# Normed rows from ScalarE with a scale and a bias per token, block 0's weights from VectorE, later counts, and a sigmoid made from exp

## The chip, the cores and the metric

The kernel runs on one core of a Trainium2 chip. The metric is the device time of one execution in microseconds; a time stands for the median of several runs. A profile is one more execution, recorded by the hardware profiler. Engines are TensorE (PE; PEld is its weight load), VectorE (DVE), ScalarE (ACT), GpSimd (POOL) and SyncE (SP, here a DMA queue).

## The reference

Eight batches of 512 tokens of 256 numbers run through four layers, each added to its input after a layer norm without weights. All is float32.

```
x = x + scan(norm(x))         # xi = silu(x @ Win + b); h = 0.9 h + xi B; y = h C + D xi; y @ Wout + b
x = x + mixture(norm(x))      # router, 16 experts, 4 chosen of each token, and two shared experts
x = x + attention(norm(x))    # 16 heads of 16, causal, scores clipped to +-10, softmax
x = x + mixture(norm(x))

# the router of a mixture:
scores = sigmoid(x @ router_w.T); s = scores + bias
group_score = sum of the 2 best of each group of 4 experts; keep the 2 best groups
topk_idx = the 4 best of s among them; tw = 2.5 * scores[topk_idx] / sum
# an expert: (silu(x @ gate) * (x @ up)) @ down, weighted by tw and summed
```

Tokens of one batch are four tiles of 128 (one token per partition). `norm` is `(x - mean) / sqrt(var + 1e-5)`.

## The kernel before, in words

The program has four stretches in time: the scan stretch (0 to about 373 us), the first mixture's routed experts (to about 770), the attention stretch (to about 1352) and the second mixture's routed experts (to 1752, then the last rows are summed and stored).

A stretch (`stretch`, L1236) goes over the batches. For each batch it issues the layer's main work (`Scan`, L492 on: `pz_s`, the input product L500, sigmoid L509, the products L510 and L513, the recurrence `state_s` L512, `y_s` L516, then `py_s`, the output product L454, which L463 adds to `x`; or `Attention`, from L1013: `pq_a`, `pv_a`, the scores `ps_a` L1096, exp by ScalarE L1107, the clip L1110 and L1118, `po_a` L1131, `pto_a` L1147). Beside the main work of batch b it issues pieces of other batches, each at a share of the main work's columns (`timed`, `spread`): the normed rows and transposes of the next batch's layer input, the routing of batch b-1 (`Route`), the shared experts of batch b-2 (L958 `pg_m`, L972 to L978, L987 `pd_m`), and the scatter of batch b-2's rows into `xg`, ordered by expert. A scheduler then orders each engine's instructions; the order of before and after is fixed when the program is built, and each engine works through its own in order. SyncE's queue carries the loads and stores, GpSimd's queue the indirect scatters.

The names that matter:

- `normed` (L405): statistics per tile (L412, L413 on VectorE), the reciprocal root `rstd` (with `by_vector`, for batches 0 and 1 of the scan layer, for the last batch's routed rows and for the attention inputs that are made beside the first mixture's blocks, by twelve small steps on VectorE, L420 to L428; else an addition on VectorE, L431, and a power on GpSimd, L432), then four rows (L437, VectorE: subtract the mean, times `rstd`). The rows are `xn` (a layer's input) or `sorted_m` (a mixture's rows, which also hold the weights and the destination).
- `turned` (L385): eight transposes by TensorE (L397) into PSUM, `pt_l` or `pt_m`, and two copies to SBUF (L399), `xT_l` or `xT_m`; in the scan layer both copies are ScalarE's.
- the router: `logits` (`pl_m`, L590, and the sigmoid L599), `choices` (VectorE, L605 to L649, ending in `sel_m`, the mask of chosen experts), the counts (`pr_m`, two matmuls with the mask, L656 and L657: how many tokens before this one chose the same expert, and how many in all), then row numbers and weights (L661 to L692), the slots (ScalarE, L703) and the scatter (GpSimd, L706).
- `blocks` (L720 to L804): which expert each block of 128 rows belongs to. TensorE counts (`pe_b`, L782, and `pl_b`, L791), ScalarE copies `expert_b` (L786).
- `routed` (L806): 136 blocks, in a pipeline. `fetch` copies a block's gate weights (ScalarE) and up weights (VectorE) out of `w_all` (L851), at a place that a register holds; `turn` transposes its rows (`pt`, L858) and ScalarE copies them (L859); `up` makes `ph` (L869), the sigmoid (ScalarE, L877), two products (VectorE, L878 and L879); `down` makes `pyr` (L897), which ScalarE scales (L905) and GpSimd adds to the sum (L906). A branch (L939) ahead of it covers counts of over 136 blocks and isn't taken.

`load_x` brings a batch's `x`; GpSimd adds the output bias to it (L487), after the statistics and the rows have read it.

Of the kernel before, what the change touches and what calls it, by code (L numbers as in the profile page):

```python
# [10 lines left out]
FP = mybir.dt.float32  # L11
# [4 lines left out]
P = 128  # L16
# [58 lines left out]
def tile_hybrid_block(  # L75
# [297 lines left out]
    def some(steps, many: int):  # L373

        for _ in range(many):
            yield next(steps)

    def issue(piece):
        for _ in piece.steps:
            pass  # L380
# [21 lines left out]
    by_both = (nc.scalar.copy, nc.vector.tensor_copy)  # L402
    by_scalar = (nc.scalar.copy, nc.scalar.copy)

    def normed(b: int, tag: str, place, by_vector: bool = False, pinned: bool = False, past=lambda: None):  # L405

        keep = tc.keep_in_program_order if pinned else lambda made: made
        x_sb = x_tiles[b]
        stats = small.tile([P, NT, 6], FP, tag="stats", name=f"stats_{tag}")
        mv = small.tile([P, NT, 2], FP, tag="mv", name=f"mv_{tag}")  # L410
        for t in range(NT):
            keep(nc.vector.bn_stats(stats[:, t, :], x_sb[:, t, :]))  # L412
            keep(nc.vector.bn_aggr(mv[:, t, :], stats[:, t, :]))  # L413
            yield
        rstd = small.tile([P, NT], FP, tag="rstd", name=f"rstd_{tag}")
        if by_vector:


            var = small.tile([P, NT], FP, tag="var", name=f"var_{tag}", bufs=1)
            keep(nc.vector.tensor_scalar(var, mv[:, :, 1], EPS, None, ALU.add))  # L420
            bits = small.tile([P, NT], I32, tag="bits", name=f"bits_{tag}", bufs=1)
            keep(nc.vector.tensor_scalar(bits, var.bitcast(I32), 1, None, ALU.logical_shift_right))
            keep(nc.vector.tensor_scalar(rstd.bitcast(I32), bits, -1.0, HALVED, ALU.mult, ALU.add))
            off = small.tile([P, NT], FP, tag="off", name=f"off_{tag}", bufs=1)
            for _ in range(3):
                keep(nc.vector.tensor_mul(off, rstd, rstd))
                keep(nc.vector.scalar_tensor_tensor(off, off, -0.5, var, ALU.mult, ALU.mult))
                keep(nc.vector.scalar_tensor_tensor(rstd, off, 1.5, rstd, ALU.add, ALU.mult))  # L428
            yield
        else:  # L430
            nc.vector.tensor_scalar(rstd, mv[:, :, 1], EPS, None, ALU.add)  # L431
            nc.gpsimd.tensor_tensor(rstd, rstd, neg_half, ALU.pow)  # L432
        xn = place()
        for t in range(NT):
            with tc.issue_after(past().ins) if past() is not None else nullcontext():
                keep(
                    nc.vector.tensor_scalar(  # L437
                        xn[:, t, :], x_sb[:, t, :], mv[:, t, 0:1], rstd[:, t : t + 1], ALU.subtract, ALU.mult
                    )
                )  # L440
            yield
# [108 lines left out]
    class Route:  # L550
# [18 lines left out]
        def norm(self, by_vector: bool = False):  # L569


            past = (lambda: gained.get(self.b - 1)) if self.i == 0 else lambda: None
            return normed(self.b, self.tag, self.place, by_vector, past=past)

        def scores(self):
            yield from turned(
# [8 lines left out]
    def logits(i: int, b: int, tag: str, held):  # L585
        xnT = held["xnT"]
        pl = bank([P, NT, E], f"pl_{tag}")
        for t in range(NT):
            for k in range(KD):
                nc.tensor.matmul(  # L590
                    pl[:, t, :],
                    lhsT=xnT[:, k, t * P : (t + 1) * P],
                    rhs=rw_sb[:, k, :],
                    start=(k == 0),
                    stop=(k == KD - 1),
                )
            yield
        score = small.tile([P, NT, E], FP, tag="score", name=f"score_{tag}")
        nc.scalar.activation(score, pl, AF.Sigmoid)  # L599
        held["score"] = score  # L600

    def choices(i: int, b: int, tag: str, held, paced: bool):
# [50 lines left out]

        pr = bank([P, 2, NT, E], f"pr_{tag}")
        flat = sel.rearrange("p t e -> p (t e)")
        nc.tensor.matmul(pr[:, 0].rearrange("p t e -> p (t e)"), lhsT=tri, rhs=flat, start=True, stop=True)  # L656
        nc.tensor.matmul(pr[:, 1].rearrange("p t e -> p (t e)"), lhsT=ones, rhs=flat, start=True, stop=True)  # L657
        row = small.tile([P, NT + 1, E], FP, tag="row", name=f"row_{tag}", bufs=3)
        nc.vector.tensor_copy(row[:, 0, :], counts[i])
        for t in range(NT):  # L660
# [145 lines left out]
    def routed(i: int, table, beside):  # L806
# [39 lines left out]
        def fetch(n: int):  # L846


            for half, (copy, name) in enumerate(((nc.scalar.copy, "gate"), (nc.vector.tensor_copy, "up"))):
                here = work.tile([P, KD * F], FP, tag="col", name=f"{name}_{i}_{n}", bufs=COLS)  # L850
                copy(here, w_all[:, bass.ds(held[n][0] + half * KD * F, KD * F)])  # L851
                held[n].append(here)

# [382 lines left out]
    def stretch(layer):  # L1236
# [5 lines left out]
        def norm(b: int, first: bool = False):  # L1242
            def place():
                xn[b] = kb4(f"xn_{i}_{b}")
                return xn[b]

            return normed(b, f"l{i}_{b}", place, first, first)

        def turn(b: int, copies=layer.copies):
            return turned(lambda: xn.pop(b), f"l{i}_{b}", lambda xnT: xT.update({b: xnT}), copies)  # L1250
# [11 lines left out]
        for b in range(layer.ahead):  # L1262
            if b < layer.early:
                if b in unturned:
                    issue(Piece(0, unturned.pop(b)))
                xT[b] = ready.pop(b)
            else:
                layer.load(b)
                first = i == 0 and b == 0
                issue(Piece(0, norm(b, first)))  # L1270
                issue(Piece(0, turn(b)))
                if first:
                    load_shared()
            if b == 0:
                issue(project(b))
# [24 lines left out]
        for b in range(1 if begun else 0, B):  # L1300
            pieces = [begun or layer.main(b, made.pop(b))]
            begun = None
            nxt, last = b + layer.ahead, b == B - 1
            fill = []
            if layer.ahead > 1 and not last:
                fill.append(project(b + 1))
            if b > 1:
                shared_sum = experts(b - 2)
                if last:

                    each = shared_sum.columns // 12
                    rest = Piece((12 - HELD) * each, shared_sum.steps)

                    many = HELD * each if layer.mixture else HELD * each * 3 // 2
                    shared_sum = Piece(many, some(shared_sum.steps, HELD))
                fill.append(shared_sum)
                pieces.append(timed(sends.pop(), 0.1, 0.14, 0.18, *spread(0.22, 0.66 if last else 0.86, NT * TK)))
            if fill:
                pieces.append(behind(*fill))
            if b > 0:  # L1320
                r = start_route(b - 1)
                if last:
                    pieces.append(timed(r.norm(), *spread(0.0, 0.12, NT), *spread(*layer.last_rows, NT)))
                else:
                    first, then, rows, full = layer.norms
                    pieces.append(timed(r.norm(), *spread(first, then, NT), *spread(rows, full, NT)))
                sends.append(r.rest)
                if last:
                    pieces += [
                        timed(r.scores(), *layer.last_scores, *spread(0.5, 0.56, NT)),  # L1330
                        timed(some(r.rest, PICKS), *spread(0.57, 0.7, PICKS)),
                        timed(some(r.rest, 3 + SENT), 0.72, 0.74, 0.76, *spread(0.78, 1.0, SENT)),
                    ]
                else:
                    pieces += [
                        timed(r.scores(), *layer.scores[:2], *spread(*layer.scores[2:], NT)),
                        timed(some(r.rest, PICKS), *spread(*layer.choose, PICKS)),
                    ]
            if nxt < B:
                added = layer.load(nxt)  # L1340
                if added is not None:
                    pieces.append(timed(added, 0.24, 0.28))
                pieces += [
                    timed(norm(nxt), *spread(0.32, 0.44, NT), *spread(0.56, 0.64, NT)),
                    timed(turn(nxt), 0.75, 0.79),
                ]
            issue(beside(*pieces))
            if layer.ahead == 1 and nxt < B:
                issue(project(nxt))
            if i == 0 and b == 2:  # L1350
                for make in pending:
                    make()
# [164 lines left out]
```

## Time and profile before

| | us |
|---|---|
| five runs | 1785.5, 1786.02, 1786.61, 1781.53, 1786.42 |
| median | 1786.02 |
| the profiled execution | 1781.09 |
| its span, first to last instruction | 1779.4 |
| mean granted TensorE clock | 0.976 of full speed |

A page of the profile gives the busy time of each engine, then the span in 40 slices of 44.5 us (each digit is the busy share in tenths; PEclk is the clock that TensorE was granted). Other views list groups of instructions by line with their mean time and the idle time ahead of them, the waits of an engine by what ended them, single instructions in order of time, and the busy time of every engine in chosen windows. Busy times are the engines' own; a matmul's end is modelled.

### The profile page before, as it was taken

To read this page: it belongs to the slowest core of one execution; us is meant where nothing else is said; L and a number is where in the kernel's file an instruction comes from. 1 tells how busy PE (TensorE), PEld (TensorE's weight loads), DVE (VectorE), ACT (ScalarE), POOL (GpSimd) and SP (SyncE) were. 2 spreads that over 40 slices of the span, in tenths; PEclk is the share of its full clock that TensorE was granted. 3 is DMA by queue.
4 is the path that set the end of the run, shared out by engine and by line. 5 is a ranking of instruction groups with operands and counts; after the bars stand their busy time and mean duration, and the time that the engine had idled before them with its cause. 6 is when DMAs were issued, how large, how long until landed. Compare 5 with 4: busy or idle time off the path is not lost. (4 is left out here: it accounts for less than half of the span.)

```text
span 1779.4 us, 32867 instructions
## 1 busy us (share of the span) xinstructions
PE 1679.0 (94%) x10640; PEld 1254.2 (70%) x10640; DVE 1095.6 (62%) x3428; ACT 806.3 (45%) x1740; POOL 769.5 (43%) x674
## 2 busy tenths in 40 slices
PE   5899996989999999999999999999998999999993
PEld 3566663579999999954545545544457999998993
DVE  8877776535555655556776676566643665555562
ACT  3223221135555555555654464454413555555551
POOL 3355553525554655530032332322451555556553
PEclk8999998999999999999999999999998999999997
DMA  4444331535555655531012211122542656666666
GB/s 156 143 165 156 131 104 56 189 80 97 94 98 103 108 97 98 102 75 37 24 41 68 77 51 64 48 79 76 170 150 66 96 95 98 107 121 135 120 129 172
DMA packets 149280, 181.38 MB, mean 102 GB/s; under 512 B 16145, under 2 KB 135985, under 8 KB 149105
## 3 DMA queue, kind: packets, MB, share of 16 engines
q0 software_dynamic: 54720, 82.57, 25.0%
q1 hardware_dynamic: 92576, 92.71, 17.6%
q10 hardware_dynamic: 1808, 3.93, 0.6%
q8 instruction: 89, 1.46, 0.3%
q14 instruction: 87, 0.70, 0.1%
HBM read 81.62 MB, written 97.53 MB: 101 GB/s over the span
## 5 line engine op out<-in xcount | busy, mean ns | idle before, releaser
L906 POOL DMA_INDIRECT part<-rows x272 | 426.1, 1567 | 338.0 <-ACT rows L905 251.4
L706 POOL DMA_INDIRECT xg<-sorted_m,slots_m x256 | 256.7, 1003 | 304.4 <-ACT slots_m L703 100.1
L869 PEld LDWEIGHTS ph<-rows,gate 128*128 128x128 f32 x2176 | 285.4, 192 | 21.0 <-ACT rows L859 6.5
L869 PE MATMUL ph<-rows,gate 128*128 128x128 f32 x2176 | 289.5, 276 | 4.9 <-ACT rows L859 4.9
L869 PE MATMUL ph<-rows,up 128*128 128x128 f32 x2176 | 288.6, 276 | 0.0
L897 PE MATMUL pyr<-w_all,rows 128*128 x1088 | 280.5, 380 | 0.6 <-DVE rstd_l L428 0.6
L869 PEld LDWEIGHTS ph<-rows,up 128*128 128x128 f32 x2176 | 266.3, 193 | 0.0
L877 ACT ACTIVATE rows<-ph 128x256 f32<-128x256 f32 x272 | 104.2, 383 | 329.7 <-PE ph L869 326.5
L878 DVE TENSOR_TENSOR rows<-ph,rows 128x256 f32<-128x256 f32 x272 | 115.1, 423 | 193.4 <-ACT rows L877 161.7
L897 PEld LDWEIGHTS pyr<-w_all,rows 128*128 128x128 f32 x1088 | 185.2, 191 | 14.9 <-ACT rows L905 1.0
L851 ACT COPY gate<-w_all 128x512 f32 x272 | 170.0, 626 | 14.8 <-PE ph L869 2.4
L1107 ACT ACTIVATE w_all<-ps_a 128x1024 f32<-128x1024 f32 x128 | 124.4, 1021 | 82.4 <-PE ps_a L1096 70.0
L851 DVE COPY up<-w_all 128x512 f32 x272 | 119.2, 439 | 30.6 <-ACTq L939 12.9
L905 ACT ACTIVATE rows<-pyr,gain 128x256 f32<-128x256 f32 x272 | 128.4, 472 | 15.0 <-PE pyr L897 13.1
L958 PE MATMUL pg_m<-xT_m,su_sb 128*128 128x512 f32 x256 | 126.3, 616 | 5.1 <-ACT expert_b L786 5.1
L1096 PE MATMUL ps_a<-w_all 32*128 32x512 f32 (+3 forms) x1024 | 122.4, 476 | 6.9 <-ACT w_all L1107 5.6
L958 PE MATMUL pg_m<-xT_m,sg_sb 128*128 128x512 f32 x256 | 125.7, 614 | 0.0
L882 DVE SCALAR_TENSOR_TENSOR gain<-rows,expert_b 128x4 f32<-128x4 f32 x272 | 60.9, 225 | 103.3 <-ACT rows L905 79.2
L987 PE MATMUL pd_m<-sd_sb,act_m 128*128 128x256 f32 x512 | 120.1, 382 | 0.9 <-DVE act_m L978 0.9
L879 DVE TENSOR_TENSOR rows<-ph,rows 128x256 f32<-128x256 f32 x272 | 115.1, 423 | 8.3
L987 PEld LDWEIGHTS pd_m<-sd_sb,act_m 128*128 128x128 f32 x512 | 95.4, 190 | 22.2 <-issue 4.7
L858 PE MATMUL pt<-ident,rows 128*128 128x128 f32 x544 | 103.7, 273 | 5.2 <-DMA rows<-xg 3.0
(219 smaller groups left out, 2210.8 us busy)
## 6 DMA issues: line engine op xcount, KB each, us to landing
rows<-xg SPq DMA_DIRECT2D x272, 136.0 KB
part<-x SPq DMA_DIRECT2D x16, 512.0 KB
part<-ys_m SPq DMA_DIRECT2D x14, 512.0 KB
w_all<-in_L_ffn_gate_w_dram SPq DMA_DIRECT2D x24, 256.0 KB
w_all<-in_L_ffn_up_w_dram SPq DMA_DIRECT2D x24, 256.0 KB
w_all<-in_L_ffn_down_w_dram SPq DMA_DIRECT2D x24, 256.0 KB
sum<-part POOLq DMA_DIRECT2D x10, 512.0 KB
xg<-zeros SPq DMA_DIRECT2D x34, 136.0 KB
```

Of the source, the lines that this page charges most:

```text
L706: nc.gpsimd.indirect_dma_start(out=xg[i], out_offset=bass.IndirectOffsetOnAxis(ap=slots[:, at : at + 1], axis=0), in_=rows[:, t, :], in_of ...
L851: copy(here, w_all[:, bass.ds(held[n][0] + half * KD * F, KD * F)])
L869: nc.tensor.matmul(ph[:, s, f * P : (f + 1) * P], lhsT=both[s][:, k * F + f * P : k * F + (f + 1) * P], rhs=rows[:, ROW + k * P : ROW + (k ...
L878: nc.vector.tensor_mul(act, ph[:, 0, :], act)
L879: nc.vector.tensor_mul(act, ph[:, 1, :], act)
L897: nc.tensor.matmul(py, lhsT=act[:, f * P : (f + 1) * P], rhs=w_all[:, bass.ds(w + 2 * KD * F + f * D, D)], start=(f == 0), stop=(f == KF - 1),
L905: nc.scalar.mul(rows[:, 0:D], py, gain[:, TK : TK + 1])
L906: nc.gpsimd.indirect_dma_start(out=parts[i][n % 2], out_offset=bass.IndirectOffsetOnAxis(ap=rows[:, D + 2 * TK : D + 2 * TK + 1].bitcast(U ...
L958: made = nc.tensor.matmul(dst, lhsT=w[:, k, f * P : (f + 1) * P], rhs=xnT[:, k, :], start=(k == 0), stop=(k == KD - 1),)
L987: nc.tensor.matmul(py[:, j, :], lhsT=acts[n][:, f, t * P : (t + 1) * P], rhs=shared[n][3][:, f, :], start=(n == 0 and f == 0), stop=(n == ...
L1096: nc.tensor.matmul(ps[j // 2][:, j % 2, col : col + n], lhsT=k_sb[w][r, o, c * P : (c + 1) * P], rhs=q_sb[r, o, c * P : T], start=True, st ...
L1107: nc.scalar.activation(es[two], ps[two][:, :, 0:cols], AF.Exp, scale=ATT_SCALE)
```

## The change

There are five edits, and the order that follows from them.

1. `normed` gets `scaled`: after `rstd`, VectorE makes `shift` = -mean * rstd (one operation on 128x4), and ScalarE writes the four rows as Identity with a scale and a bias per token. It is used for the scan layer's input of batches 1, 2 and 3, and for the first mixture's rows of batches 0 and 1. There, an order that kept those rows behind an operation of the previous batch (`past`) is dropped.
2. The second transposed copy of the very first batch goes from ScalarE to VectorE.
3. The second mixture's scores are made by exp of -x (ScalarE), a minimum with an addition of 1, and a reciprocal (VectorE), in place of the sigmoid.
4. The counts of the last batch but one (`pr_m` of batch 6, in both stretches) are issued after the last matmul of the shared experts issued so far (`wide`), and the times at which the last passes issue the fifth pick and the steps after it are later.
5. Block 0's gate and up weights are both copied by VectorE, into a tile of `xpool`.
The order of the instructions of the two stretches and of the start of the routed experts follows from these. On SyncE it is unchanged, on GpSimd only one early memset moves; from batch 3 of the scan stretch on, TensorE, VectorE and ScalarE keep their order there, and `pr_m` of batch 6 stays between the two `py_s` groups of batch 7. In the attention `pr_m` of batch 6 moves behind the next group of `po_a`, and clip operations of VectorE come ahead of the picks. Fifteen of ScalarE's table loads are gone from the attention, two are added at the start of the second mixture's blocks; at the start of both mixtures the loads of a register for block 0 come ahead of the branch, and ScalarE copies the gate weights of blocks 1, 2 and 3 ahead of block 0's rows, where it copied those of 0, 1 and 2.

```diff
+        if scaled:
+            bias = small.tile([P, NT], FP, tag="shift", name=f"shift_{tag}")
+            nc.vector.scalar_tensor_tensor(bias, mv[:, :, 0], -1.0, rstd, ALU.mult, ALU.mult)
+            for t in range(NT):
+                nc.scalar.activation(
+                    xn[:, t, :], x_sb[:, t, :], AF.Identity, bias=bias[:, t : t + 1], scale=rstd[:, t : t + 1]
+                )
+                yield
+            return
...
-            return normed(self.b, self.tag, self.place, by_vector, past=past)
+            return normed(self.b, self.tag, self.place, by_vector, past=past, scaled=self.i == 0 and self.b < 2)
...
-        nc.scalar.activation(score, pl, AF.Sigmoid)
+        if i == 0:
+            nc.scalar.activation(score, pl, AF.Sigmoid)
+        else:
+            nc.scalar.activation(score, pl, AF.Exp, scale=-1.0)
+            nc.vector.tensor_scalar(score, score, 3.0e38, 1.0, ALU.min, ALU.add)
+            nc.vector.reciprocal(score, score)
...
-        nc.tensor.matmul(pr[:, 0].rearrange("p t e -> p (t e)"), lhsT=tri, rhs=flat, start=True, stop=True)
-        nc.tensor.matmul(pr[:, 1].rearrange("p t e -> p (t e)"), lhsT=ones, rhs=flat, start=True, stop=True)
+        with tc.issue_after(wide[-1].ins) if b == B - 2 else nullcontext():
+            nc.tensor.matmul(pr[:, 0].rearrange("p t e -> p (t e)"), lhsT=tri, rhs=flat, start=True, stop=True)
+            nc.tensor.matmul(pr[:, 1].rearrange("p t e -> p (t e)"), lhsT=ones, rhs=flat, start=True, stop=True)
...
+            if n == 0:
+                both = xpool.tile([P, NT, D], FP, tag="x", name=f"both_{i}").rearrange("p t d -> p (t d)")
             for half, (copy, name) in enumerate(((nc.scalar.copy, "gate"), (nc.vector.tensor_copy, "up"))):
-                here = work.tile([P, KD * F], FP, tag="col", name=f"{name}_{i}_{n}", bufs=COLS)
+                if n == 0:
+                    here = both[:, half * KD * F : (half + 1) * KD * F]
+                    copy = nc.vector.tensor_copy
+                else:
+                    here = work.tile([P, KD * F], FP, tag="col", name=f"{name}_{i}_{n}", bufs=COLS)
                 copy(here, w_all[:, bass.ds(held[n][0] + half * KD * F, KD * F)])
...
-            return normed(b, f"l{i}_{b}", place, first, first)
+            return normed(b, f"l{i}_{b}", place, first, first, scaled=i == 0 and 0 < b < 4)
...
-                issue(Piece(0, turn(b)))
+                issue(Piece(0, turn(b, by_both if first else layer.copies)))
...
-                        timed(some(r.rest, PICKS), *spread(0.57, 0.7, PICKS)),
-                        timed(some(r.rest, 3 + SENT), 0.72, 0.74, 0.76, *spread(0.78, 1.0, SENT)),
+                        timed(some(r.rest, PICKS), *spread(0.57, 0.67, PICKS - 1), 0.76),
+                        timed(some(r.rest, 3 + SENT), 0.79, 0.81, 0.83, *spread(0.85, 1.0, SENT)),
```

More of the change, by code (lines that the diff above doesn't have):

```diff
@@ L403, in tile_hybrid_block, with normed @@
     by_scalar = (nc.scalar.copy, nc.scalar.copy)
-    def normed(b: int, tag: str, place, by_vector: bool = False, pinned: bool = False, past=lambda: None):
+    def normed(
+        b: int, tag: str, place, by_vector: bool = False, pinned: bool = False, past=lambda: None, scaled: bool = False
+    ):
         keep = tc.keep_in_program_order if pinned else lambda made: made
```

## The prediction

> **What bounds the kernel now.** I read the page first: which engine is busy, and where not.
>
> ```profile
> span 1779.4 us, 32867 instructions
> PE 1679.0 (94%) x10640; PEld 1254.2 (70%) x10640; DVE 1095.6 (62%) x3428; ACT 806.3 (45%) x1740; POOL 769.5 (43%) x674
> PE   5899996989999999999999999999998999999993
> PEclk8999998999999999999999999999998999999997
> ```
>
> TensorE is the bound. Its 100 us of idle time lie in the first two slices, slice 6 (the scan stretch's end), slice 30 (the attention's end) and the last. The change can win only where TensorE waits or runs at a lowered clock, so the waits of TensorE came next:
>
> ```profile
> PE pr_m L656 <- DVE sel_m L649: 17.4, 3, 13.6
> PE pt_l L397 <- DVE xn L437: 9.8, 1, 9.8
> PE pt_m L397 <- DVE sorted_m L437: 8.8, 8, 3.0
> PE pz_s L500 <- ACT xT_l L399: 8.0, 1, 8.0
> PE ps_a L1096 <- ACT w_all L1107: 5.6, 12, 1.0
> PE ph L869 <- ACT rows L859: 4.9, 4, 2.2
> ```
>
> Columns: total us, times, longest. The 9.8 is the input's arrival and the first norm, which stay. The table by windows (length, busy time of PE, PEld, DVE, ACT, POOL, then the clock) shows where the clock falls after such waits:
>
> ```profile
> 24.00:36.00 12.00, 7.18 (x11) 3.13 (x12) 8.64 (x10) 5.09 (x9) 0.00 (x0) 0.57 0.01 2
> 36.00:82.00 46.00, 41.20 (x152) 26.34 (x151) 41.31 (x124) 13.80 (x26) 10.11 (x13) 0.96 0.29 95
> 290.00:308.00 18.00, 4.47 (x14) 3.85 (x15) 6.19 (x35) 0.38 (x3) 6.73 (x7) 0.62 0.18 63
> 1262.00:1280.00 18.00, 14.22 (x90) 6.55 (x88) 13.09 (x59) 7.12 (x14) 6.15 (x6) 0.81 0.59 188
> ```
>
> The granted clock is 0.57, 0.62 and 0.81 there. The lowered stretches in the clock's record last 3.41 us or a multiple of it (82.14 to 85.55, 1269.98 to 1276.81), and each costs up to half its length.
>
> **The change, part by part.** The terms are against the profiled execution, 1781.09 us (span 1779.4); the median of the five runs, 1786.02, is 4.9 above it, and I add that at the end.
>
> *Rows by ScalarE, price.* The timeline of VectorE and two ScalarE groups give it:
>
> ```profile
> 50.64 1.39 DVE L437 TENSOR_SCALAR sorted_m<-x,mv_m,rstd_m 128x256 f32<-128x256 f32 x4 [1.09 <-POOL rstd_m L432]
> 54.26 2.20 DVE L437 TENSOR_SCALAR xn<-x,mv_l,rstd_l 128x256 f32<-128x256 f32 x4
> L877 ACT ACTIVATE rows<-ph 128x256 f32<-128x256 f32 x272 | 104.2, 383 | 329.7 <-PE ph L869 326.5
> L905 ACT ACTIVATE rows<-pyr,gain 128x256 f32<-128x256 f32 x272 | 128.4, 472 | 15.0 <-PE pyr L897 13.1
> ```
>
> VectorE takes 1.39 us for four rows, 2.20 beside GpSimd's adds. ScalarE takes 383 ns without and 472 with one operand per row; I estimate 560 with two (bounds 472 to 660), some 2.0 us for four in a row. Moving five norms frees 1.39 to 2.20 us of VectorE each; the shift operation (128x4, about 0.17) is added each time.
>
> The Trainium skill speaks against this: "ScalarE: Activation LUTs", section Rules for kernel authors, gives multiplications and additions to VectorE. The rows agree that each row gets dearer; by the rule alone this part would lose some 0.6 us a norm.
>
> *Batch 1 at launch.* Before, VectorE ends xn_1 at 18.85, but the transposed copies on ScalarE start only at 28.20, behind scan 0's multiplications, and pz_s of batch 1 starts at 28.82. In the changed order VectorE also makes a transposed copy of batch 0 (0.69) after TensorE's transposes (ready 12.04), so batch 1's statistics start about 2.2 us later. The three integer steps cost 0.65 each beside GpSimd's adds and about 0.2 once those are over (-1.4), but three xi/state pairs (0.74 + 1.22 each) lie inside the root's chain. That ends it near 23.7; four rows on ScalarE to 26, transposes, a sigmoid and a copy: pz_s near 27. Gain about 1.6; later in batch 1 ScalarE's sigmoids and TensorE set the pace, and it stays.
>
> *Batch 0's routed rows.* The root leaves GpSimd 1.6 earlier, then shift 0.2 and a first row 0.15 slower: the transposes gain about 1.2, the fourth row 0.7. I take 1.0.
>
> *Later counts of batch 0 and batch 1's rows.* xn_2 leaves VectorE (2.2), but the shifts are queued behind GpSimd's powers (1.02 to 1.05 each, in pairs), and sel_m of batch 0 is queued behind the shifts of batches 1 and 3. In before it ends at 65.5 and its pr_m issues at 67.73, 2.2 of cover. Two powers in order cost 2.1 less the work left; with TensorE earlier too I expect up to 1.1 of wait at pr_m. The timeline of TensorE has
>
> ```profile
> 79.30 0.33 PE L397 MATMUL pt_m<-ident,sorted_m 128*128 128x128 f32 x1 [0.66 <-DVE sorted_m L437]
> 80.74 0.65 PE L397 MATMUL pt_m<-ident,sorted_m 128*128 128x128 f32 x2 [1.11 <-DVE sorted_m L437]
> ```
>
> and both waits go, since ScalarE writes these rows some 10 us earlier: -1.8, and the lowered clock at 82.14, half of 3.41, -1.7. The steady period of 39.9 us per batch is TensorE's; batches 2 to 6 keep their order.
>
> Launch in all: -1.0 (batch 1's 1.6 seen through the wait for the routed rows), +1.1, -1.8, -1.7: -3.4. Ends: -6 (no wait at pr_m, clock up earlier in 24 to 34) and +2 (ScalarE's rows behind its scan work hold up TensorE where VectorE's did not).
>
> *Counts of batch 6.* The long stall, 13.6 us before pr_m in the scan stretch, is not touched: the changed kernel keeps pr_m directly between the two py_s groups there, and TensorE's result of 289.95 reaches VectorE only after GpSimd's unbroken row of scatters (278.3 to 298.6), which the change does not alter. In the attention pr_m goes behind another group of po_a. Before:
>
> ```profile
> 1270.14 0.69 PE L656 MATMUL pr_m<-sel_m,tri 128*128 128x64 f32 x2 [2.99 <-DVE sel_m L649]
> ```
>
> With clip operations now ahead, sel_m should end 1.2 later, with about 2.4 us of TensorE work in between at full clock; a wait of 0.9 stays. That saves 2.1, and the lowered clock after it (po_a takes 3.64 where an earlier batch shows 1.93) another 1.5: -3.6, between 0 (another gap takes its place) and -7 (both stretches of 3.41 go). GpSimd idles 10.72 before the last scatters at 1313.76, so 1.2 later counts are covered there.
>
> *Sigmoid from exp.*
>
> ```profile
> L599 ACT ACT_TABLE_LOAD x8 | 10.3, 1283 | 0.1
> L1107 ACT ACT_TABLE_LOAD x8 | 10.3, 1283 | 6.2 <-PE ps_a L1096 5.6 <-issue 0.6
> ```
>
> Fifteen of these sixteen go, 19 us of ScalarE; but TensorE's waits for the exponentials are 5.6 in all, and those within 4 us after a load (at 866.34, 867.25, 1265.88) sum to 0.8. I take -1 (0 to -2). VectorE gets two small operations per batch, about 0.4, hidden except for the last batch, where the score chain is what everybody waits for: +0.2. "ScalarE: Activation LUTs", section What ACT_TABLE_LOAD costs, puts every switch at 2.66 us, the load and a drain; fifteen would be 40 us, and the trace shows that off the path they are worth about 1.
>
> *Block 0's weights.* Three gate copies of 0.55 stood ahead of rows_0 on ScalarE, and they still do (those of blocks 1, 2, 3 instead of 0, 1, 2). Only a register load comes earlier, about -0.6 at 374. In the second mixture a table load comes back ahead of the copies, since the last function before is now exp: +1.28 - 0.6 = +0.7. A second load falls into ScalarE's 3.45 us of idle time before 1359.05. If that cover goes, +1.3.
>
> Sum: -3.4 - 3.6 - 1 + 0.2 - 0.6 + 0.7 = -7.7: 1773.4 on the profile's scale, 1778.3 on the median's.
>
> **Rivals.**
>
> *Given back, no change.* The launch is VectorE's until 50 and the powers, waited for in order, eat the freed time; the launch gives 0 and the attention 2.1 without the clock. With the rest (-0.7) that is -2.8: 1783.2. For it: two powers per pair of shifts, on a VectorE that is busy 41 of 46 us. Against it: its work there does shrink.
>
> *Slower.* TensorE's result stuck behind GpSimd's scatters, as at 303.53, a second time, in the attention. It needs the scatters of batch 5 or 6 to run unbroken (0.30 between them) while VectorE waits for a result of TensorE; before, ScalarE's slots break them up (2.0 to 2.4 us between pairs at 1242 to 1253). Freed of table loads ScalarE delivers slots closer together, which is for it; that all sixteen would have to be ready is against it. It decides from a row of about 10 scatters on. Price: at least that of 303.53, 13.6 plus half a clock stretch of 3.4: +15.3 - 7.7 = +7.6, 1793.6; with half the row, 1787 to 1790.
>
> *More.* The shift of the launch moves scatters and py_s so that the stall of 13.6 goes, with its clock (13.65 at half): -15 more, 1763. Against it: the same order on every engine there.
>
> **Numbers.** Forecast (launch and attention both pay) 0.50, more 0.08, given back 0.22, slower 0.20. About 3.6 us (0.2%) is what a measurement of this kernel can tell from no change; its own runs spread over 5. Faster 0.60 (forecast, more, and a little of given back), same 0.19, slower 0.21. The forecast's own range, by its ends, is 1771 to 1784; 8 in 10 need 1769 to 1790.
>
> **What would show it.** Right: pz_s of batch 1 near 27, no waits for sorted_m at 79 to 81 on the shifted clock, fewer lowered stretches in 1262 to 1280, one table load in the attention, ScalarE's rows of 0.47 to 0.56. Wrong: the stall of 13.6 gone or doubled, waits of over 1.5 at pr_m of batch 0, ScalarE ahead of TensorE at launch, or a wait for rows of over 3.5 at the second mixture's start.

## The result, and the profile after

| | median us | runs |
|---|---|---|
| before | 1787.44 (1778.76 to 1797.75) | 89 |
| changed | 1785.51 (1776.77 to 1793.03) | 51 |
| changed, profiled execution | 1782.25, span 1780.5 | 1 |

The ratio is 0.9987 (95% interval 0.998 to 0.9995): 1.9 us by the medians, 2.3 by the ratio. It has the predicted sign, but is under the 0.2% that counts as a change here, and between a quarter and a third of the 7.7 that were forecast. The median of 1785.51 lies outside the forecast's own range (1771 to 1784) and inside the wide one (1769 to 1790).

The page of the changed kernel:

```profile
span 1780.5 us, 32882 instructions
PE 1681.1 (94%) x10640; PEld 1256.6 (71%) x10640; DVE 1091.5 (61%) x3432; ACT 797.8 (45%) x1744; POOL 771.1 (43%) x674
PE   6899996999999999999999999999999999999993
PEclk9899998999999999999999999999999999999997
```

Slices 0, 8 and 30 are fuller than before by a tenth; slices 1, 6 and the last are as they were. The clock is up in slices 0 and 30 and down in slice 1. TensorE's waits (total us, times, longest):

```profile
PE pr_m L675 <- DVE sel_m L667: 15.4, 4, 13.8
PE pt L884 <- DMA rows<-xg: 7.0, 5, 2.7
PE ps_a L1122 <- ACT w_all L1133: 5.7, 11, 1.0
PE ph L895 <- ACT rows L885: 5.5, 4, 3.1
PE pt_m L397 <- DVE sorted_m L449: 4.0, 5, 0.8
PE pt_m L397 <- ACT sorted_m L441: 3.3, 1, 3.3
PE pt_l L397 <- ACT xn L441: 3.1, 1, 3.1
```

The 8.0 before pz_s has become 3.1 before pt_l. The 3.0 before the first sorted_m has become 3.3. The 13.8 is still there, and the wait for rows at a mixture's start has grown from 2.2 to 3.1. The windows (length, busy time of PE, PEld, DVE, ACT, POOL, then the clock):

```profile
24.00:36.00 12.00, 11.19 (x29) 5.48 (x30) 10.62 (x12) 7.02 (x13) 3.68 (x4) 0.86 0.02 6
36.00:82.00 46.00, 41.77 (x145) 27.49 (x144) 32.18 (x110) 17.09 (x34) 7.07 (x10) 0.89 0.47 155
290.00:308.00 18.00, 5.87 (x20) 5.09 (x21) 5.68 (x27) 0.38 (x3) 6.06 (x7) 0.62 0.16 53
1262.00:1280.00 18.00, 14.50 (x94) 8.15 (x93) 13.56 (x54) 5.83 (x12) 5.19 (x6) 1.00 0.76 247
```

The clock is up from 0.57 to 0.86 and from 0.81 to 1.00, but down from 0.96 to 0.89 in 36 to 82. This execution starts the second mixture's first block at 1348.71, 6.7 us ahead of before, and is 1.1 us longer at the end: the wait for loads of rows has grown from 3.0 to 7.0, all of it in the blocks beside which sums are loaded (the five waits end between 1593.6 and 1702.6). So my first theory was that these loads give the gain back.

### The profile page after: what moved, and what is told of

The parts are those of the page before. It is cut to its first block, busy times and chain, and to the rows that moved or that the text cites. A ratio compares the mean times of both kernels' runs of the same rounds, so it can differ in the third digit from the quotient of the medians.

```text
span 1780.5 us, 32882 instructions
## 1 busy us (share of the span) xinstructions
PE 1681.1 (94%) x10640; PEld 1256.6 (71%) x10640; DVE 1091.5 (61%) x3432; ACT 797.8 (45%) x1744; POOL 771.1 (43%) x674
```

## The experiments

Sets of kernels ran together, each beside runs of before. Line numbers of after hold for all but kernels made from before.

**First set: is the gain lost beside the sums? (before 1762.84)** In two kernels the five early sums are added at the end:

```diff
-            return {
-                SUMMED[b]: [lambda: sums.update({b: sum_of(b, homes, beside)})],
-                SUMMED[b] + 8: [lambda: add_up(b, sums.pop(b), beside)],
-            }
+            return {}
...
-        with tc.If(again > 0):
-            for b in SUMMED:
-                at_the_end(b)
         for b in range(B):
-            if b not in SUMMED:
-                at_the_end(b)
+            at_the_end(b)
```

> The kernel of before with the sums of batches 0 to 4, which are loaded and added beside the second mixture's blocks, moved to the end with those of batches 5 to 7. Theory 1 (the change's gain of 6.7 us at the start of the second mixture is real in most executions, and the blocks give it back because the loads of rows wait behind the 512 KB loads of the sums): no wait of TensorE for the loads of rows in the second mixture (before 2.6 us in the profile), runs that spread by less than the 1779 to 1798 of before; the time itself is longer than before by the five sums at the end, about 20 to 35 us by the 27 us that three sums and the drain take there now. Theory 2 (the gain of 6.7 us is not typical; other executions of before reach the second mixture earlier or those of after later): the same time, but the spread stays.

> The changed kernel with the same edit. Theory 1: 5 to 8 us below the kernel of before with that edit. Theory 2: 1 to 3 us below it, as the whole change. The profile should show the first block of the second mixture near 1348.7 under theory 1; under theory 2 at a place that differs by some microseconds from the profile of after.

no_scaled drops `scaled=...` from both calls and `by_both if first else` from the first turn:

> The changed kernel without ScalarE's rows and with the first batch's copies as before (edits 1 and 2 undone). By the two profiles the launch gained 1.5 us (pr_m of batch 1 and all later batches): theory 1 and 2 both expect 1 to 2 us slower than the changed kernel. A rival (the launch's clock is a matter of chance; in after it was lowered for 10.2 us at 50 to 60, which cost about 3.4 us more than in before): 3 to 5 us slower.

old_counts takes out `issue_after(wide[-1].ins)` and puts the four old times back:

> The changed kernel with pr_m of batch 6 and the times of the picks as before (edit 4 undone). By the profiles the attention's end gave 2.7 us at pr_m of batch 6 and 1.5 at expert_b: theory 1: the first block of the second mixture about 4 us later than in the profile of after, and 0 to 4 us slower in all, as the blocks give back more or less; theory 2: no difference over 1 us.

| kernel | median us | ratio to before (95%) |
|---|---|---|
| before_sums_last | 1770.00 | 1.0035 (1.0022 to 1.0049) |
| after_sums_last | 1761.10 | 0.9986 (0.9971 to 1.0001) |
| no_scaled (7 runs) | 1753.51 | 0.9950 (0.9928 to 0.9972) |
| old_counts | 1757.97 | 0.9967 (0.9951 to 0.9983) |

With the sums at the end the change is worth 8.9 us (1770.00 - 1761.10), as theory 1 said. But before itself took 1762.8 in this set, 24.6 below its 1787.4, and even the version without ScalarE's rows won 9.3. Had the sums at the end cost the changed kernel the 7.2 us that they cost before (1770.00 - 1762.84), it would have taken about 1753.9 in this set (an estimate): no_scaled is level with that, where 1 to 2 us more were expected, and old_counts is 4 us above it, as theory 1 had it. The profiles showed why before was so much shorter. VectorE in the kernel of before, at the scan stretch's long stall:

```profile
290.52 0.16 DVE L633 MAX8 best_m<-s_m 128x8 f32<-128x16 f32 x1
300.96 0.69 DVE L463 TENSOR_TENSOR x<-py_s,x 128x512 f32<-128x512 f32 x1 [10.28 <-remote]
```

and in before_sums_last, which is the same kernel up to there:

```profile
290.93 0.16 DVE L633 MAX8 best_m<-s_m 128x8 f32<-128x16 f32 x1
291.01 0.67 DVE L463 TENSOR_TENSOR x<-py_s,x 128x512 f32<-128x512 f32 x1
```

In both GpSimd is in the middle of its scatters (278 to 299 and on). In the one, TensorE's finished py_s is seen by VectorE only 2.4 us after the last scatter of the row ends (298.57); in the other at once, while the row goes on. So a third theory: the gain is lost where TensorE's results come late beside GpSimd's scatters. I call sets "late" or "prompt" by this, with a wait at pr_m of batch 6 of about 13.8 or 3.4 us. The prompt sets are the first and the fifth; the sets with after's own runs were all late. It is no property of a chip: the first and the fourth set ran on the same one.

**Second set, late (before 1786.65): the parts alone.** after_again is the changed kernel; scaled_alone is before with edits 1 and 2, counts_alone before with edit 4; old_fetch is the changed kernel with `n == 0` made false in `fetch`.

> The changed kernel once more, beside the kernel of before. In the runs so far a kernel whose long stall at pr_m of batch 6 in the scan stretch takes 3.4 us in place of 13.7 reached the first mixture some 10 to 12 us earlier, before and after alike. Theory 1 (the blocks of the second mixture give the gain back through waits for the loads of rows): 1 to 3 us below before, with waits for rows of over 5 us. Theory 3 (the gain goes only where the stall behind GpSimd's scatters is long; without it the change brings what was forecast): 7 to 9 us below before when pr_m of batch 6 in the scan stretch waits about 3 us, 1 to 3 us below when it waits about 13.6.

> The kernel of before with edits 1 and 2 alone (ScalarE's rows and the first copies). By the profiles 1.5 to 3.8 us earlier from batch 1 on: theories 1 and 3 expect 1 to 4 us below before. The rival (it is worth nothing or costs, since the version without it was 9.3 us below before): 0 to 3 us above before.

> The kernel of before with edit 4 alone (later counts of batch 6). Theory 3: 3 to 5 us below before. Theory 1: 0 to 3 us below, with more wait for the loads of rows than before. In both pr_m of batch 6 in the attention waits about 1.4 us in place of 3 to 4.

> The changed kernel with block 0's weights copied as before (edit 5 undone). By the profiles the start of the first mixture is 0.5 us later, that of the second as in after within 0.5: all theories expect 0 to 1 us slower than the changed kernel, which these runs can hardly tell; a rival (the tile that block 0 takes out of the pool of x tiles delays the loads of the sums or of the next layer's inputs): 2 to 4 us faster than the changed kernel.

| kernel | median us | ratio to before (95%) |
|---|---|---|
| after_again | 1783.94 | 0.9985 (0.9969 to 1.0002) |
| scaled_alone | 1784.05 | 0.9977 (0.9956 to 0.9999) |
| counts_alone | 1784.55 | 0.9997 (0.9979 to 1.0015) |
| old_fetch | 1783.52 | 0.9986 (0.9969 to 1.0003) |

The launch's part alone brings about what the whole does; the later counts alone nothing that can be measured: theory 3 had 3 to 5 us for them, a miss, although pr_m of batch 6 waits 0.68 in counts_alone where scaled_alone, with the old counts, shows 2.99. The fetch makes no difference. Each interval is about 3 us either way, so the parts can't be summed from here. after_again's waits for rows were 1.9 us, not over 5, and its profiled execution was the slowest of its twelve runs (1787.41): its front is what is late. TensorE and VectorE of after_again show a wait that neither before nor after has:

```profile
355.58 0.69 DVE L1004 TENSOR_TENSOR act_m<-pg_m,sig_m 128x512 f32<-128x512 f32 x1 [2.86 <-remote]
```

```profile
357.41 2.28 PE L801 MATMUL pe_b<-chosen_b,cand_e 128*128 128x143 f32 x8 [3.00 <-DVE chosen_b L790]
```

A matmul's result is seen 2.86 us late, again inside GpSimd's scatters (of batch 7); chosen_b is queued behind it on VectorE, and TensorE waits for that.

**Third set, late (before 1794.83): theory 1 against theory 3.**

> The changed kernel a third time. The four kernels of the first set of runs ran where the stall at pr_m of batch 6 in the scan stretch is 3.4 us and before takes 1762.8; those of the second where it is 13.8 and before takes 1786.7. If this set runs where the stall is short: theory 1 (waits for rows beside the sums give the gain back) says 1 to 3 us below before, theory 3 (the gain is lost only where results of TensorE come late beside GpSimd's scatters) says 7 to 10 us below. Where the stall is long: both say 1 to 4 us below.

> The kernel of before with all sums at the end, again. Both theories: about 7 us above before, as in the first set.

> The changed kernel with all sums at the end, again; 8.9 us below the kernel of before with that edit in the first set. Where the stall is long: theory 1 says 7 to 9 us below it again, theory 3 says 1 to 4 us. Where the stall is short: both say 7 to 9.

> The changed kernel without ScalarE's rows and with the first copies as before, again; it was 8.4 us below before where the stall is short (7 runs). Where the stall is long: theory 3 says 0 to 3 us below before, theory 1 says 6 to 9. Against the changed kernel beside it: ScalarE's rows are worth 1 to 4 us by the profiles, so it should be that much slower; if it isn't, the launch's part brings nothing.

| kernel | median us | ratio to before (95%) |
|---|---|---|
| after_third | 1789.06 | 0.9973 (0.9942 to 1.0004) |
| before_sums_last_2 | 1801.09 | 1.0031 (1.0007 to 1.0054) |
| after_sums_last_2 | 1797.51 | 1.0019 (0.9992 to 1.0046) |
| no_scaled_2 | 1794.23 | 0.9995 (0.9971 to 1.0019) |

Theory 1 falls: in a late set, with no sums beside the blocks the change is worth 3.6 us (by the means of 12 runs each 2.7, standard error 1.9), not 8.9 (standard error 1.1). The kernel without ScalarE's rows, 8.4 to 9.3 below before in the prompt set, is level with it here. It was expected 1 to 4 us above the changed kernel, and is above it: 1794.23 beside 1789.06, by the means 4.4 with a standard error of 2.3, which is not clear of noise. In the prompt profiles the launches with and without edits 1 and 2 differ by 2.5 us. The changed kernel as such ran in no prompt set, so what it would take beside the first set's no_scaled was not seen; the estimate above makes them level. after_sums_last_2's profile has the wait at pe_b at 6.61 us.

**Fourth set, late (before 1785.85): are the scatters the cause?** late_sends moves batch 5's scatters behind pr_m of batch 6 in the scan stretch, early_sends brings them ahead of the copy that pto_a waits for in the attention, both_sends does both:

```diff
-pieces.append(timed(sends.pop(), 0.1, 0.14, 0.18, *spread(0.22, 0.66 if last else 0.86, NT * TK)))
+# late_sends
+pieces.append(timed(sends.pop(), 0.1, 0.14, 0.18, *(spread(0.93, 1.0, NT * TK) if last and i == 0 else spread(0.22, 0.66 if last else 0.86, NT * TK))))
+# early_sends
+pieces.append(timed(sends.pop(), 0.1, 0.14, 0.18, *spread(0.22, (0.48 if i else 0.66) if last else 0.86, NT * TK)))
```

> The changed kernel with the scatters of batch 5 in the scan stretch's last pass issued later (at 0.93 to 1.0 of the pass in place of 0.22 to 0.66), so that they come after pr_m of batch 6. Theory 3 (TensorE's results come late while GpSimd runs its unbroken scatters; no scatter runs when py_s ends near 290): pr_m of batch 6 waits about 3.4 us in place of 13.8 and all later work of that stretch is 10 us earlier; 6 to 14 us below the changed kernel, less what the now unbroken 48 scatters hold up later (they need 61 us from about 298, so they would end near 361 as now, just at the first mixture's start). The rival (the stall has another cause, the choices of batch 6 on VectorE for example): it stays at 13.8, 0 to 5 us slower. Where the stall is short already, within 3 us of the changed kernel.

> The changed kernel with the scatters of batch 5 in the attention's last pass issued earlier (0.22 to 0.48 in place of 0.22 to 0.66 of the pass), so that they end before ScalarE's copy of oT at the place where pto_a now waits (1.1 to 3.5 us in four profiles where the stall is long, 1.5 where it is short). Theory 3: that wait is 1.5 or less, and pr_m of batch 6 comes 11 to 12 us after the 960th po_a matmul, as where the stall is short, in place of 13.0 to 14.6; 1 to 3 us below the changed kernel. The rival (the wait is ScalarE's own work): no change.

> Both edits of the two kernels above. Theory 3: their sum, 7 to 16 us below the changed kernel, and 10 to 18 below before. The rival: no better than the changed kernel.

> The changed kernel beside them: 2 to 5 us below before where the stall is long; where it is short (before near 1763), 7 to 10 below.

| kernel | median us | ratio to before (95%) |
|---|---|---|
| late_sends | 1793.09 | 1.0038 (1.0021 to 1.0055) |
| early_sends | 1781.10 | 0.9979 (0.9963 to 0.9995) |
| both_sends | 1790.03 | 1.0027 (1.0012 to 1.0042) |
| after_fourth | 1782.77 | 0.9980 (0.9964 to 0.9996) |

TensorE of late_sends:

```profile
291.38 0.43 PE L675 MATMUL pr_m<-sel_m,tri 128*128 128x64 f32 x2 [3.04 <-DVE sel_m L667]
291.66 0.39 PE L676 MATMUL pr_m<-sel_m,ones 128*128 128x64 f32 x2
...
322.80 2.28 PE L397 MATMUL pt_m<-ident,sorted_m 128*128 128x128 f32 x8 [18.68 <-DVE sorted_m L449]
```

With no scatter running, the wait of 13.8 is 3.04 in a late set: that stall needs the scatters. They are not enough for it, since in the prompt sets the same row of scatters runs without it. But the kernel is 10 us slower than the changed one, for a reason that my expectation missed, and both_sends, expected 7 to 16 us below the changed kernel, is 7 above it. VectorE shows it:

```profile
322.34 1.47 DVE L449 TENSOR_SCALAR sorted_m<-x,mv_m,rstd_m 128x256 f32<-128x256 f32 x4 [19.88 <-DMA xg<-sorted_m,slots_m]
```

The rows of batch 7 go into the buffer that batch 5's scatters read (the pool holds two), so scatters that are moved back hold up the next rows. early_sends took the wait at pto_a to 1.14 and pr_m of batch 6 to 11.3 us after the 960th po_a matmul, as expected (13.6 in after_fourth), but it gains no time that this measurement can tell: 1781.10 beside 1782.77.

**Fifth set, prompt (before 1764.28): the table loads.** best is early_sends with the sigmoid kept for the last batch (`if i == 0 or b == B - 1`), so that ScalarE ends the attention with the sigmoid's table; sigmoid keeps it for all batches.

> The changed kernel with early_sends' edit, and with the sigmoid kept for the last batch's scores of the second mixture, so that ScalarE ends the attention with the sigmoid's table. If the table load ahead of the gate copies is what makes TensorE wait 3.31 us there (before 2.40) and keeps its clock down for 6.8 us in place of 3.4: the wait falls to 1.7 to 2.1, the clock is down for 3.4 us or not at all, and the start of the second mixture with its first 31 blocks is 1.5 to 2.5 us shorter than in the changed kernel; 2 to 4 us below it in all, 5 to 8 below before. If not, no change there.

> The changed kernel with the sigmoid in the second mixture's scores (edit 3 undone): fifteen table loads are back in the attention, none at the second mixture's start. By the profiles the attention up to its 400th score matmul is 1.1 to 1.3 us longer (184.2 in place of 182.9), the second mixture's start 0.9 to 2 us shorter: in all within 1.5 us of the changed kernel, 2 to 5 us below before where the stall is long, 7 to 10 where it is short. A rival (the loads cost the attention what the Trainium skill's price makes of them, 2.66 us each): 10 us or more slower.

| kernel (6 runs) | median us | ratio to before (95%) |
|---|---|---|
| best | 1752.32 | 0.9929 (0.9906 to 0.9953) |
| sigmoid | 1751.68 | 0.9930 (0.9913 to 0.9946) |

ScalarE of after at the second mixture's start, then TensorE of after, and then TensorE of best:

```profile
1345.44 1.28 ACT L877 ACT_TABLE_LOAD   x1 [0.79 <-DVE gain L908]
1346.73 1.66 ACT L877 COPY gate<-w_all 128x512 f32 x3
1348.30 0.64 ACT L885 COPY rows<-pt 128x256 f32<-128x256 f32 x2
```

```profile
1348.71 3.57 PE L895 MATMUL ph<-rows,both 128*128 128x128 f32 x15 [3.15 <-ACT rows L885]
```

```profile
1329.44 2.05 PE L895 MATMUL ph<-rows,both 128*128 128x128 f32 x16 [1.86 <-ACT rows L885]
```

The wait falls from 3.15 to 1.86, the clock stays up, and from the first ph to the ph 31 blocks later it takes 87.7 us where the prompt profile of the change (after_sums_last) has 90.3 and before_sums_last 89.4. With the start itself (from expert_b's end to the first ph, 18.7 to 17.4) that is 3.9 us for one table load of 1.28. The other two prompt profiles with that load, no_scaled and old_counts, take 89.9 and 89.3 from the same start; against them it is 3.5 and 2.9. Undoing the exp for all batches is as good: the ordinary loads are worth 1.1 us in all (the table in the next section). Both kernels beat before by more than was expected of them (12.0 and 12.6 us, where 5 to 8 and 7 to 10 were) and by more than the changed kernel does anywhere, but the changed kernel did not run in their set, so by how much they beat it is not measured.

## Why the prediction was wrong, point by point

Times between fixed matmuls, from the profiles: late, two of before's order against five of the changed; prompt, before_sums_last against after_sums_last. The numbers of ps_a and po_a matmuls count from 0. Differences in us:

| from, to | step of the prediction | forecast | late | prompt |
|---|---|---|---|---|
| start to batch 2's sorted_m | launch | -3.4 | -1.3 | -3.8 |
| pr_m of batch 7 to pe_b, scan stretch | none | 0 | +1.9 | 0.0 |
| pe_b to the first block | block 0's weights | -0.6 | -0.3 | -0.6 |
| attention to the 400th ps_a | table loads | -1 | -1.1 | -1.2 |
| to the 960th po_a | none | 0 | +1.4 | -1.9 |
| 960th to 1016th po_a | counts, wait and clock | -3.6 | -2.2 | -4.1 |
| to pr_m of batch 7 | batch 7's scores | +0.2 | +1.1 | -1.4 |
| behind expert_b's wait, to the first block | table load, second mixture | +0.7 | +0.7 | +0.9 |
| first 31 blocks | none | 0 | +1.0 | +0.9 |

**The launch** went by the steps up to 48 us: pz_s of batch 1 at 26.57 (27 forecast), the waits at 79 to 81 and the clock at 82 gone, powers waited for in order (1.09 and 0.96, then 1.00 and 0.95), a wait of 0.46 at pr_m of batch 0 where up to 1.1 was allowed. ScalarE's rows took 585 to 612 ns, not 560, and above the 0.47 to 0.56 that were to show it right. The first transposes of sorted_m come 2.8 us earlier (48.38 against 51.21), where 1.0 was taken; those of batch 2's inputs come 0.4 earlier (57.89 against 58.26). The mis-sized term is the clock in between: TensorE still waits 3.3 us for the first sorted_m, and after that the clock is down for 10.24 us where before had 3.41, so that the same four py_s take 2.05 in place of 1.11. TensorE of before, and then of after:

```profile
51.21 0.30 PE L397 MATMUL pt_m<-ident,sorted_m 128*128 128x128 f32 x1 [3.03 <-DVE sorted_m L437]
54.89 1.11 PE L454 MATMUL py_s<-w_scan,y_s 128*128 128x256 f32 x4
```

```profile
48.38 0.33 PE L397 MATMUL pt_m<-ident,sorted_m 128*128 128x128 f32 x1 [3.30 <-ACT sorted_m L441]
51.35 2.05 PE L466 MATMUL py_s<-w_scan,y_s 128*128 128x256 f32 x4
```

I counted the stretch at 82 as gone and left the one at 51 as it was. "TensorE: Matmul & The Clock Gate", Part 1 of the Trainium skill, says that the clock halves after an idle window of about 3.4 us and that the window runs freely; the lengths here (3.41, 6.83, 10.24) agree, but the waits that TensorE has ahead of them are shorter than that, 3.30 here and 2.24 at the second mixture's start of before. The five late profiles of the changed kernel gain between 0.5 and 2.5, and the 3.8 of the prompt pair was good luck: over all 14 profiles with the changed launch batch 2's rows are turned at 119.1 on average (117.6 to 120.5), over the six with the old one at 120.6 (120.0 to 121.4), a gain of 1.5 where 3.4 were forecast.

**The counts**: the step itself was right. In after and in the prompt profile of the change pr_m of batch 6 waits 0.9 to 1.0 and po_a's 24 matmuls take 1.93; the prompt pair gives -4.1. TensorE of after:

```profile
1267.04 1.93 PE L1157 MATMUL po_a<-w_all,v_a 128*32 128x512 f32 x24
1269.96 0.41 PE L675 MATMUL pr_m<-sel_m,tri 128*128 128x64 f32 x2 [0.99 <-DVE sel_m L667]
```

In the other four late profiles pr_m does not wait, but pto_a, which now stands ahead of it, waits 0.7 to 3.1 us, and the 24 matmuls, at a lowered clock, take 2.9 to 3.4. TensorE's timeline of after_third, the longest of these waits:

```profile
1271.34 0.66 PE L1173 MATMUL pto_a<-ident,oT_a 128*128 128x128 f32 x4 [3.13 <-ACT oT_a L1170]
```

The exp ahead of that copy on ScalarE had itself waited 3.74 us for a result of TensorE and began 1.1 us after the last scatter of batch 5, and po_a's 24 matmuls took 3.39. In early_sends, where these scatters are over by then, the wait is 1.14 and the 24 matmuls take 1.93.

**The failed step** is the sum. It added up each gain as if all of it reached the end, and put at nothing every wait and every lowered clock between the places that it named. The sentence that the long stall "is not touched" held: the stall is 13.6 and 12.1 in the two profiles of before and 13.7 to 13.8 in the five of the changed kernel, and the launch's gain passes it (-1.3 ahead of it, -1.4 at pr_m of batch 7). What failed are sizes: the launch, -3.4 in the sum, is -1.3 in the late profiles, by the clock; the counts, -3.6, are -2.2, by the wait at pto_a and the clock behind it; and places that stood at nothing took the rest, +1.9 ahead of pe_b, +1.4 before po_a's 960th matmul, 0.9 more than forecast around batch 7's scores and +1.0 in the first blocks.

The stall is one of a kind: in late sets results of TensorE are seen late at several places beside scatters (pto_a, pe_b, expert_b, pr_m), and the places and sizes differ from run to run. I read this so: a gain ahead of such a place is kept only if the late result isn't the next thing waited for. That lateness costs the gain is shown as a whole, by the 8.9 us with prompt results and 2.7 to 3.6 with late ones, both with the sums at the end. Which place took how much is read from profiles alone: the +1.9 comes from two of the five (2.9 and 6.5), only two profiles of before stand against them, and early_sends, which took one such wait away, gained nothing that can be measured.

The late column sums to about 0 at the second mixture's start (mean 1355.8 for the five against 1356.2 for the two; the largest difference that the table doesn't list is -0.5 at expert_b); the profile of after with its 1348.7 was a lucky one. In the prompt pair the difference there is 14.9 us, chance of the clock included (-2.6 of it lies in the first mixture's blocks, which the table doesn't list), and 8.9 by the timed runs. The rival "given back" named the right size (-2.8) by luck, with VectorE's powers as its cause; the late results are the mechanism of the slower rival, in small pieces. I had asked for a row of ten scatters as the point from which it decides; the 3.1 us at pto_a came beside rows of six and four.

**The table loads**: -1.1 and -1.2, as forecast (-1), and all of it by the 400th ps_a, where four loads go. The next six gave 0.0; the last five lie where the clock and the counts differ too. The one that came back costs 1.7 to 1.8 over the start and the first blocks, forecast 0.7. The missing part is the clock: behind a wait of 3.15 it is down for 6.8 us (for 3.4 in old_counts and early_sends), behind 2.24 (before) for 3.4, and not at all behind 1.86 (best, sigmoid). The wait alone does not decide it: at the first mixture's start the clock goes down for 3.4 us behind 1.78 in after, and stays up behind 1.79 in after_sums_last. Against the kernels of the fifth set the load costs 2.9 to 3.9, against the 1.1 that the other loads were worth: so the exp in place of the sigmoid gains nothing, and the sigmoid kernel, as fast as best, agrees.

**The loads of rows** beside the sums vary between 1.1 and 7.0 us of wait in four profiles of the changed kernel; that is part of the spread of the runs, and no step of mine.

Open: why two sets are prompt. In the profiles of those sets nearly every semaphore update of TensorE has its record (1771 to 1777), in the late ones 1289 to 1428; whether recording and lateness have one cause, what besides the scatters makes a set late, and whether an unrecorded execution is late, these runs can't show. The 1.4 us before the 960th po_a come from three of the five profiles; the clock is down at 1230 to 1252 in all seven, in these three for longer or later.

## What to carry to other kernels

A gain is worth what is left of it at the next wait: list the waits downstream by what ends them, and price a gain ahead of a wait whose end is set elsewhere (a GpSimd queue, a DMA) at nothing until an experiment says more. Price a wait of TensorE as itself plus a range for the clock behind it: here waits of 2.2 to 3.3 us were followed by 3.4 to 13.7 us of lowered clock, in profiles of one and the same kernel by different lengths. One table load on the path cost more (2.9 to 3.9 us) than fifteen off it saved (1.1).

## What the runs showed of the hardware that I had not expected

In three of the five sets, and in the first profiles of before and after, finished TensorE results were seen late by VectorE or ScalarE while GpSimd issued indirect scatters back to back (0.96 us each, 0.30 apart). At the scan stretch's stall VectorE waited 8.6 to 10.3 us for one in all twelve late profiles whose scatters were not moved, until 2.4 to 2.7 us after the last scatter of the row; in after_again another came 2.9 us late in the middle of a row. In the other two sets the same result came at once, and the kernel of before was 21 to 32 us shorter. An Identity on ScalarE with a scale and a bias per partition takes 585 to 612 ns for 128x256.
